# One of q's seven block products split again into seven products of blocks of half the size

## The chip, the cores and the metric

The kernel runs on one core of a Trainium2 chip. The metric is the device time in microseconds (us) of one execution. Besides that time there is a profile of one execution, in which every instruction has a start and a duration. Its engines are PE (TensorE, matrix products; PEld is the loading of its weights), DVE (VectorE), ACT (ScalarE), POOL (GpSimd) and SP (the engine that issues the DMAs here).

## The reference

Two graph layers on 64 batch elements of 256 nodes and 512 features, all in float32. The change touches one step of the second layer, the projection of its normalised input to queries.

```
h = maximum(_layernorm(x), 0)                 # x: (64, 256, 512)
x = x + concatenate([alpha @ (h @ W), h @ W]) # layer 0, alpha = masked softmax of a[0], a[1] scores
h = maximum(_layernorm(x), 0)
q = split_heads(h @ Wq.T + bq)                # 8 heads of 64
k = split_heads(h @ Wk.T + bk)
v = split_heads(h @ Wv.T + bv)
scores = einsum('bhqd,bhkd->bhqk', q, k) / 8;  masked by adj, softmax
x = x + (attn @ v merged) @ Wo.T + bo
```

## The kernel before

**Groups and stages.** The 64 batch elements are taken in 32 groups of two (`GB = 2`, `NG = 32`), so a group has 512 tokens. Three groups are in flight at once. While group g is in attention, group g+1 is projected to q, k and v (`project`, L850), and group g+2 goes through the first layer (`first_layer`, L705). The order is written out by hand in two strings (`steps`, L1182), one for each batch element b of group g. Each letter takes one piece of work: S scores, m one multiplication of softmax weights by the mask, u one product of the projection, s one piece of the first layer, o one product of the output projection, n a piece of normalisation, f a piece of the row sums ("fold"). The string for b = 0 begins `Smmnfuuuumonmnuofuusssosff`, so the seven products of q (the first seven u) stand in it, and right behind them the first products of the first layer (s).

**Order on the engines.** The matrix products run in the order in which they are written (`in_order`, L131). On VectorE, ScalarE and GpSimd, `not_sooner` (L123) keeps an instruction behind the one written before it; a scheduler places the rest. Nearly all lines of a profile read L137 (`matmul`) or L35 (every other operation), so they are told apart by the names of tiles.

**A product as seven products of half-size blocks.** q of one group is a 512 x 512 matrix times 512 tokens. It is cut into four blocks by halves of the inner dimension and of the tokens, and computed by seven products of 256 x 256 blocks instead of eight (`projection`, L857; `seven`, L534; the sums of the weights in `weight_sums`, L253). Product i multiplies one of the operands a11, a12, s4, a22, s1, s2, s3 by one of seven forms of the weight. The sums s1, s2, s3 (written over a21) and s4 come from four subtractions and additions on GpSimd (`operand_sums`, L525), named `sums` and `hT` in the profile. The products are made in the order 1, 2, 6, 7, 5, 4, 3. Products 1, 6, 5 and 3 add up in one PSUM bank, `first`, and 7 and 4 in another, `second`. In between, ScalarE copies partial results out (`kept`, L904) and VectorE adds them to the outputs:

```
L927        product(second, 4, False)
L928        vector.tensor_add(part(1, 0), second, p16)
L930        product(first, 3, False)
L931        take(part(0, 1), first, 1)
```

One such product is four matmul calls of a 128 x 128 weight by 256 columns. A float32 call leaves two records in the profile, so it is a run of 8 records. Product 3 of q has the weight block `W22`, the operand s4, and is shown as `pq<-sums,wq_sb`. `take` is two activations on ScalarE (`q<-pq,bq_sb`), which add the bias.

**What follows in the same stretch.** The first layer's products (`first_products`, L636, tile `ph`) have the same shape of scheme with 129 columns: in the order 1, 2, 6, 7, 5, 4, 3, `first` holding 1, 6, 5, 3. Before product 3 may add to `first`, VectorE must have taken product 5 out of it (L694, `H<-ph,kept_h`). Their operand sums (tiles `sums_r`, `sums_xn`, `hT`) are four more operations on GpSimd.

**VectorE and GpSimd around it.** For each batch element VectorE multiplies the softmax weights by the mask in four instructions of 128x1024 (`mask_pairs`, L970, `p<-p,maskT`). GpSimd adds the two halves of each (L983, `p<-p`). The sums of the softmax rows go through DRAM and come back as `parts` (`fold`, L990): GpSimd adds `parts` in two instructions (L1016), VectorE transposes and reduces them (L1020 to L1023). GpSimd's order in this stretch is: four `sums` operations, four `p<-p` additions, four operations for the first layer, two `parts` additions.

**Rings of buffers.** `mm` (L109) takes one of 5 PSUM banks in turn, `held_bank` (L112) a bank of its own. The tag `kept` has 3 SBUF buffers in turn.

Of the kernel before, what the change touches and what calls it, by code (L numbers as in the profile page):

```python
# [14 lines left out]
P = 128  # L15
# [42 lines left out]
def bounded(  # L58
# [37 lines left out]
    NQ = D // DH // QH  # L96
    S = 32
    scale = 1.0 / DH**0.5

    const = ctx.enter_context(tc.tile_pool(name="const", bufs=1))  # L100
    big = ctx.enter_context(tc.tile_pool(name="big", bufs=2))
# [56 lines left out]

    load(0, 0)

    square_ones = const.tile([P, P], F32, name="square_ones")
    gpsimd.memset(square_ones, 1.0)
    ident = const.tile([P, P], F32, name="ident")
    make_identity(nc, ident)
    maskT = const.tile([P, NT, N], mybir.dt.uint8, name="maskT")
    bad = const.tile([P, 2, NT], F32, name="bad")
# [86 lines left out]
    def weight_sums(name, engine=vector):  # L253
        w = w_sb[name]
        not_sooner(engine, "tensor_sub", w[:, :, T3, :], w[:, :, W22, :], w[:, :, W12, :])
        engine.tensor_sub(w[:, :, T1, :], w[:, :, W12, :], w[:, :, W11, :])
        engine.tensor_sub(w[:, :, T2, :], w[:, :, W22, :], w[:, :, T1, :])
        engine.tensor_sub(w[:, :, T4, :], w[:, :, W21, :], w[:, :, T2, :])

    def first_weight_sums():  # L260
        w11, w12, w21, w22 = (
# [31 lines left out]
    def judge():  # L293

        part = const.tile([P, 10], F32, name="part")
        vector.memset(part, 0.0)
        room = att.tile([P, 2 * HP + 1, P], F32, tag="p", name="room", bufs=1)  # L300
        heads = room[:, 2 * HP, :]
        vector.memset(heads, 0.0)
        for j in range(2):
            vector.memset(heads[j * DH : (j + 1) * DH, j * DH : (j + 1) * DH], 1.0)
        power = {}

        def bank(name):
            return mm(name).rearrange("p (h o) -> p h o", h=HP)

        for n, name in enumerate(("q", "k")):  # L310
            gram = bank(f"gram_{name}")
            for hp in range(HP):
                half, cols = hp // 2, slice(hp % 2 * P, (hp % 2 + 1) * P)
                for c in range(HP):
                    w = w_sb[name][:, c % 2, c // 2 * 2 + half, cols]
                    matmul(gram[:, hp, :], w, w, start=(c == 0), stop=(c == HP - 1))
            power[name] = room[:, n * HP : (n + 1) * HP, :]
            not_sooner(
                vector, "tensor_mul", power[name], gram, heads[:, None, :].to_broadcast([P, HP, P])
            )  # L320
            yield
        squared = {}
        for i in range(2):
            for n, name in enumerate(("q", "k")):
                square = bank(f"square_{name}{i}")
                for hp in range(HP):
                    a = power[name][:, hp, :]
                    matmul(square[:, hp, :], a, a, start=True, stop=True)
                if i < 1:
                    squared[name] = square  # L330
                else:
                    scalar.activation(
                        power[name], square, AF.Square, accum_out=part[:, 8 + n : 9 + n]
                    )
                yield
            for name, square in squared.items():
                not_sooner(scalar, "copy", power[name], square)
            if squared:
                squared.clear()
                yield  # L340

        def squares(col, *srcs):
            sums = small.tile([P, HP], F32, tag="sums", name=f"sums{col}", bufs=2)
            room = att.tile([P, D], F32, tag="kept", name=f"squares{col}", bufs=3)
            for i, src in enumerate(srcs):
                to = room[:, : src.free_size()]
                if len(src.shape) == 3:
                    to = to.rearrange("p (a b) -> p a b", a=src.shape[1])
                not_sooner(
                    scalar, "activation", to, src, AF.Square, accum_out=sums[:, i : i + 1]  # L350
                )
            vector.reduce_sum(part[:, col : col + 1], sums[:, : len(srcs)], axis=AX.X)

        squares(2, *[w0_sb[:, c, :] for c in range(HP)])
        yield
        squares(3, *[w_sb["v"][:, :, i, :] for i in range(HP)])
        yield
        for i in range(2):
            squares(i, w0_sb[:, :, i])
        yield  # L360
        squares(4, bcol["q"])
        squares(5, bcol["k"])
        squares(6, bv_col)
        vector.reduce_max(part[:, 7:8], bad.rearrange("p a t -> p (a t)"), axis=AX.X)
        yield
        total = mm("total")[:, :10]
        matmul(total, square_ones, part, start=True, stop=True)
        norm = const.tile([P, 10], F32, name="norm")
        vector.tensor_scalar(norm, total, 1e-30, None, op0=ALU.add)
        power = const.tile([P, 10], F32, name="power")  # L370
        gpsimd.memset(power, 0.5)
        gpsimd.memset(power[:, 7:8], 1.0)
        gpsimd.memset(power[:, 8:10], 1.0 / 16)
        gpsimd.tensor_tensor(norm, norm, power, op=ALU.pow)
        norms_found.append(norm)
        yield
# [3 lines left out]
    def conclude():  # L380
        (norm,) = norms_found
        root = float(D) ** 0.5


        changed = 3.0**0.5

        test = const.tile([P, 5], F32, name="test")
        side = const.tile([P, 2], F32, name="side")
# [23 lines left out]
        held = const.tile([P, 1], F32, name="held")  # L412
# [444 lines left out]
    def projection(g, name, ops):  # L857
# [69 lines left out]
        product(second, 4, False)  # L927
        vector.tensor_add(part(1, 0), second, p16)  # L928
        yield
        product(first, 3, False)  # L930
        take(part(0, 1), first, 1)  # L931
        yield

    def value_differences(g, b):
# [202 lines left out]
    def run(part):  # L1137
        for _ in part:
            pass
# [44 lines left out]
    for g in range(NG):  # L1184
        products = project(g + 1) if g + 1 < NG else iter(())
        pieces = first_layer(g + 2) if g + 2 < NG else iter(())
        for b, parts in enumerate(steps):
# [10 lines left out]
            i, count = -1, sum(part not in "frv" for part in parts)  # L1198
            for part in parts:
                i += part not in "frv"  # L1200
                if part == "u":
                    next(products, None)
# [4 lines left out]
                elif part == "n":  # L1207
                    next(norms, None)
                elif part == "m":
                    next(masks)  # L1210
                elif part == "f":
                    next(folds, None)
                    continue
                elif part == "r":
                    next(additions, None)
                    continue
                elif part == "v":
                    if g < NG - 1:
                        value_differences(g, b)
                    continue  # L1220
                else:
                    waiting = (g, b, scores(g, b))
                    masks = mask_pairs(waiting[2], g == NG - 1)
                    folds = fold(*waiting)
# [6 lines left out]
                        load(g + 3, b)  # L1231
                if b == 1 and i == 8 and g >= 2:
                    next(verdict, None)
        run(products)
        run(pieces)
    run(late)
# [5 lines left out]
def any_inputs(  # L1242
# [27 lines left out]
    TOK = GB * N  # L1270
    NG = B // GB
    scale = 1.0 / DH**0.5

    const = ctx.enter_context(tc.tile_pool(name="any_const", bufs=1))
    setup = ctx.enter_context(tc.tile_pool(name="any_setup", bufs=1))
# [333 lines left out]
```

## Time and profile before

| what | value |
|---|---|
| time, median of 3 runs | 2383.98 us (2383.02 to 2384.33) |
| time of the profiled execution | 2383.11 us |
| its span in the profile | 2381.5 us |
| PE busy | 2369.8 us (100%) |
| PEld busy | 1998.5 us (84%) |
| DVE busy | 1695.2 us (71%), 3347 instructions |
| POOL busy | 1421.3 us (60%), 1288 instructions |
| ACT busy | 1016.6 us (43%) |
| granted TensorE clock | 1.0 |

The span is what lies between the first and the last instruction; the profiled execution's own time is 1.6 us more. Each row of a timeline gives the start in us from the start of the span, the duration in us, the engine, the line, the operation, the tiles written and read, the shape and the number of merged instructions; a bracket at the end gives the engine's idle time before it and what ended it. PE's busy time is a modelled one: a run of 8 records of 256 columns is shown as 1.89 us, and the next run starts 1.73 us after it.

### The profile page before, as it was taken

The page shows a single profiled execution, that of the slowest core. Times are in us where ns is not written, and L with a number is a line of the kernel's source. Part 1 is how long each engine was busy: PE and PEld are TensorE (multiplying, and loading weights), DVE is VectorE, ACT ScalarE, POOL GpSimd, SP SyncE. Part 2 cuts the span into 40 slices and gives each one's busy share as a digit, 9 for nine tenths or more (in the row PEclk, how much of TensorE's full clock was granted, in tenths as well). Part 3 has the DMA queues.
Part 4 walks back from the last instruction along what each step waited for, and adds up shares of the span by engine and source line. Part 5 has one row for each costly group of instructions (what it writes and reads, how often), then busy time and mean ns, then how long its engine had stood idle before and what let it go on. Part 6 is the DMA issues. An engine that isn't in the chain of part 4 may idle for free.

```text
span 2381.5 us, 43080 instructions
## 1 busy us (share of the span) xinstructions
PE 2369.8 (100%) x15828; PEld 1998.5 (84%) x15828; DVE 1695.2 (71%) x3347; ACT 1016.6 (43%) x2017; POOL 1421.3 (60%) x1288
## 2 busy tenths in 40 slices
PE   9999999999999999999999999999999999999998
PEld 8888888888888888888888888888888888888886
DVE  7577676776766776767777667776677676677666
ACT  5444444443443444444444434444444444343431
POOL 4575665666656555666656575566665565656551
PEclk9999999999999999999999999999999999999999
DMA  5344445444445544454444455444544445554331
GB/s 186 128 148 146 140 137 162 151 150 149 138 141 157 167 146 138 138 157 154 142 147 142 151 155 168 141 136 139 162 151 147 141 143 156 153 157 146 110 106 46
DMA packets 271865, 343.50 MB, mean 144 GB/s; under 512 B 25376, under 2 KB 217120, under 8 KB 271648
## 3 DMA queue, kind: packets, MB, share of 16 engines
q1 hardware_dynamic: 271648, 340.69, 46.2%
q8 instruction: 126, 2.06, 0.4%
q14 instruction: 91, 0.75, 0.1%
HBM read 176.95 MB, written 163.64 MB: 143 GB/s over the span
## 4 chain that ended last, share of the span: by engine, by line
PE 97%; DVE 1%; POOL 1%; DMA 1%; issue 0%; ACT 0%; SPq 0%; ACTq 0%; POOLq 0%; DVEq 0%
PE pq L137 16%; PE pk L137 16%; PE py L137 16%; PE pv L137 16%; PE sc L137 10%; PE pr L137 9%; PE ph L137 8%; PE po L137 5%; DMA x<-in_x_dram 0%; POOL parts L35 0%; PE total L137 0%; DVE x L35 0%; PE gram_q L137 0%; PE gram_k L137 0%; DVE prod L35 0%
## 5 line engine op out<-in xcount | busy, mean ns | idle before, releaser
L35 POOL TENSOR_TENSOR p<-p 128x512 f32<-128x512 f32 x248 | 388.3, 1579 | 460.2 <-DVE p L35 456.5
L35 DVE TENSOR_TENSOR p<-p,maskT 128x1024 f32<-128x1024 f32 x256 | 333.1, 1322 | 3.2 <-ACT p L35 3.2
L35 ACT ACTIVATE p<-sc 128x512 f32<-128x512 f32 x512 | 257.8, 627 | 148.8 <-PE sc L137 144.1
L35 DVE TENSOR_TENSOR x<-py,x 128x256 f32<-128x256 f32 x448 | 185.1, 413 | 186.4 <-PE py L137 180.2
L35 ACT ACTIVATE xn<-x,factor 128x512 f32<-128x512 f32 x256 | 194.7, 807 | 284.1 <-POOL factor L35 276.6
L35 POOL TENSOR_TENSOR parts<-parts 128x512 f32<-128x512 f32 x248 | 247.7, 999 | 74.0 <-DMA parts<-rows 52.1
L137 PE MATMUL py<-wo_sb,oT 128*128 128x256 f32 x1024 | 262.4, 379 | 0.6 <-DVE oT L35 0.6
L137 PE MATMUL pk<-hT,wk_sb 128*128 128x256 f32 x1024 | 244.8, 382 | 0.0
L137 PE MATMUL pq<-hT,wq_sb 128*128 128x256 f32 x1024 | 240.1, 382 | 1.1 <-ACT hT L35 0.7
L137 PE MATMUL sc<-q,k 64*128 64x256 f32 x2048 | 239.5, 383 | 0.1
L137 PE MATMUL pv<-wv_sb,hT 128*128 128x256 f32 x1024 | 236.8, 379 | 0.0
L137 PE MATMUL pr<-p,v 128*32 128x256 f32 x4096 | 234.2, 380 | 0.0
L137 PEld LDWEIGHTS sc<-q,k 64*128 64x128 f32 x2048 | 193.3, 187 | 46.8 <-issue 26.3
L35 POOL TENSOR_TENSOR factor<-factor,rexp 128x2 f32<-128x2 f32 (+1 forms) x132 | 118.0, 894 | 187.3 <-DVE factor L35 187.0
L137 PEld LDWEIGHTS pq<-hT,wq_sb 128*128 128x128 f32 x1024 | 191.8, 190 | 36.7 <-issue 10.3
L137 PEld LDWEIGHTS py<-wo_sb,oT 128*128 128x128 f32 x1024 | 194.2, 190 | 28.2 <-DVE oT L35 1.1
L137 PEld LDWEIGHTS pk<-hT,wk_sb 128*128 128x128 f32 x1024 | 189.7, 190 | 33.3 <-issue 9.9
L137 PEld LDWEIGHTS pv<-wv_sb,hT 128*128 128x128 f32 x1024 | 194.6, 190 | 26.5
L137 PEld LDWEIGHTS pr<-p,v 128*32 128x32 f32 x4096 | 126.7, 110 | 97.8 <-issue 15.9
L137 PE MATMUL py<-wo_sb,o_sums 128*128 128x256 f32 x768 | 197.6, 380 | 0.5 <-DVE x L35 0.5
L137 PE MATMUL pv<-wv_sb,sums 128*128 128x256 f32 x768 | 181.6, 379 | 0.3 <-DVE v L35 0.3
L137 PE MATMUL pk<-sums,wk_sb 128*128 128x256 f32 x768 | 181.5, 379 | 0.0
(149 smaller groups left out, 4058.7 us busy)
## 6 DMA issues: line engine op xcount, KB each, us to landing
passed<-xt SPq DMA_DIRECT2D x124, 512.0 KB, 3.1
moved<-passed SPq DMA_DIRECT2D x496, 128.0 KB, 3.4
rows<-p SPq DMA_DIRECT2D x124, 512.0 KB, 3.4
parts<-rows SPq DMA_DIRECT2D x496, 128.0 KB, 3.0
x<-in_x_dram SPq DMA_DIRECT2D x64, 512.0 KB, 4.4
out_dram<-x SPq DMA_DIRECT2D x62, 512.0 KB, 4.0
own<-line SPq DMA_DIRECT2D x30, 256.0 KB, 3.1
wq_sb<-in_L_gnn_Wq_dram SPq DMA_DIRECT2D x2, 512.0 KB, 9.2
```

Source lines behind the costliest of these rows:

```text
L35: instruction = getattr(self.engine, operation)(*args, **kwargs)
L137: in_order(nc.tensor.matmul(*args, **kwargs))
```

## The change

From group 2 on (`FINER = 2`), product 3 of q alone is made by seven products of 128 x 128 blocks, by the same scheme once more. Its operand s4 and its weight `W22` are cut into four blocks each. What is new:

- `finer_weight_sums` makes three sums of blocks of the weight and writes a fourth over one of them: four VectorE instructions of 128x128, once, in group 0 at b = 1.
- `finer_sums` makes four sums of blocks of the operand, four VectorE instructions of 128x128 in each group, at the third mask multiplication of b = 0 (the m after four u).
- `finer_product` replaces `product(first, 3)` and `take`. Products 2, 4 and 3 of the small blocks add straight onto quarters of `first`. Products 1 and 7 go to a new PSUM bank, and ScalarE copies both out in one instruction (128x256, tile `saved_q`). Product 6 is added onto product 1 in that bank and copied (128x128), then product 5, and copied. VectorE adds the copies, the bias and `first` in two instructions of 128x256, and the seventh product with a third. `saved_q` is a fourth buffer per group of the ring `kept`.
- `tails` puts small product 6 behind the first s after the seventh u, and small product 5 behind the second s.

Apart from this, the constants `square_ones` and `ident` move to one tile, `early`, that shares its place with a later one, and a few small tiles of the check on the inputs shrink from 128 to 32 partitions.

```diff
-    square_ones = const.tile([P, P], F32, name="square_ones")
+    early = big.tile([P, 2, P], F32, tag="oT1", name="early", bufs=1)
+    square_ones, ident = early[:, 0], early[:, 1]
...
+    def finer_weight_sums(name):
+        w11, w12, w21, w22 = finer_blocks(name)
+        made = big.tile([P, 3, P], F32, tag="finer", name=f"finer_{name}", bufs=1)
+        t1, t2, t4 = (made[:, i] for i in range(3))
+        not_sooner(vector, "tensor_sub", t1, w12, w11)
+        vector.tensor_sub(t2, w22, t1)
+        vector.tensor_sub(t4, w21, t2)
+        not_sooner(vector, "tensor_sub", w12, w22, w12)
+        finer[name] = {1: w11, 2: w21, 3: w22, 4: t4, 5: t1, 6: t2, 7: w12}
...
+    def finer_sums(g, s4):
+        a11, a12, a21, a22 = (
+            s4[:, c, m * P : (m + 1) * P] for m in range(2) for c in range(2)
+        )
+        sums = big.tile([P, 4, P], F32, tag="s4", name=f"s4_{g}", bufs=1)
+        s1, s2, s3, s4 = (sums[:, i] for i in range(4))
+        not_sooner(vector, "tensor_add", s1, a21, a22)
+        not_sooner(vector, "tensor_sub", s2, s1, a11)
+        not_sooner(vector, "tensor_sub", s3, a11, a21)
+        not_sooner(vector, "tensor_sub", s4, a12, s2)
+        finer_operands[g] = {1: a11, 2: a12, 3: s4, 4: a22, 5: s1, 6: s2, 7: s3}
+        yield
...
+        if name == "q" and g >= FINER:
+            tail = finer_product(g, name, first, part(0, 1))
+            next(tail)
+            tails.append([tail, 2, 1, 2])
+            yield
+            return
         product(first, 3, False)
         take(part(0, 1), first, 1)
...
+    def finer_product(g, name, first, to):
+        weights, by = finer[name], finer_operands[g]
+        bank = mm(f"p{name}3_{g}")
+        x1, x7 = bank[:, :P], bank[:, P : 2 * P]
...
+        saved = att.tile([P, 4, P], F32, tag="kept", name=f"saved_{name}_{g}", bufs=3)
...
+        product(quarter(first, 0, 0), 2)
+        product(quarter(first, 0, 1), 4)
+        product(quarter(first, 1, 0), 3)
+        product(x1, 1, True)
+        product(x7, 7)
+        scalar.copy(saved[:, :2].rearrange("p i n -> p (i n)"), bank[:, : 2 * P])
+        yield
+        product(x1, 6)
+        scalar.copy(saved[:, 2], x1)
+        yield
+        product(x1, 5)
+        scalar.copy(saved[:, 3], x1)
+        for o, made in ((0, saved[:, 0:3:2]), (1, saved[:, None, 3].to_broadcast([P, 2, P]))):
+            both = [of[:, o].rearrange("p (m n) -> p m n", m=2) for of in (to, first)]
+            add(both[0], o, both[1], made)
+        upper = to[:, :, P:]
+        vector.tensor_add(upper, upper, saved[:, None, 1].to_broadcast([P, 2, P]))
+        yield
...
+                if (g, b) == (FINER - 2, 1) and part in "suo" and i == 20:
+                    finer_weight_sums("q")
...
                 elif part == "m":
                     next(masks)
+                    if i >= 4:
+                        next(fine, None)
...
+                if part in "suo" and tails:
+                    tail = tails[0]
+                    tail[1] -= 1
+                    if tail[1] == 0:
+                        next(tail[0])
+                        tail[1] = tail[2]
+                        tail[3] -= 1
+                    if tail[3] == 0:
+                        tails.pop(0)
```

More of the change, by code (lines that the diff above doesn't have):

```diff
@@ L98, in bounded @@
     scale = 1.0 / DH**0.5
+    FINER = 2
     const = ctx.enter_context(tc.tile_pool(name="const", bufs=1))
@@ L159, in bounded @@
     load(0, 0)
-    square_ones = const.tile([P, P], F32, name="square_ones")
+    early = big.tile([P, 2, P], F32, tag="oT1", name="early", bufs=1)
+    square_ones, ident = early[:, 0], early[:, 1]
     gpsimd.memset(square_ones, 1.0)
-    ident = const.tile([P, P], F32, name="ident")
     make_identity(nc, ident)
@@ L258, in weight_sums, with finer_blocks @@
         engine.tensor_sub(w[:, :, T4, :], w[:, :, W21, :], w[:, :, T2, :])
+    finer = {}
+    def finer_blocks(name):
+        w = w_sb[name][:, :, W22, :]
+        return [w[:, c, o * P : (o + 1) * P] for c in range(2) for o in range(2)]
+    def finer_weight_sums(name):
[7 more added lines that the diff above has]
+        finer[name] = {1: w11, 2: w21, 3: w22, 4: t4, 5: t1, 6: t2, 7: w12}
+    finer_operands = {}
+    def finer_sums(g, s4):
[10 more added lines that the diff above has]
+        yield
+    tails = []
     def first_weight_sums():
@@ L365, in judge @@
         yield
-        total = mm("total")[:, :10]
-        matmul(total, square_ones, part, start=True, stop=True)
-        norm = const.tile([P, 10], F32, name="norm")
+        total = mm("total")[:S, :10]
+        matmul(total, ones, part, start=True, stop=True)
+        norm = const.tile([S, 10], F32, name="norm")
         vector.tensor_scalar(norm, total, 1e-30, None, op0=ALU.add)
-        power = const.tile([P, 10], F32, name="power")
+        power = const.tile([S, 10], F32, name="power")
         gpsimd.memset(power, 0.5)
@@ L385, in conclude @@
         changed = 3.0**0.5
-        test = const.tile([P, 5], F32, name="test")
-        side = const.tile([P, 2], F32, name="side")
+        test = const.tile([S, 5], F32, name="test")
+        side = const.tile([S, 2], F32, name="side")
         not_sooner(vector, "tensor_add", test[:, 0:1], norm[:, 0:1], norm[:, 1:2])
@@ L411, in conclude @@
         vector.tensor_scalar(test, test, 1.0, None, op0=ALU.is_le)
-        held = const.tile([P, 1], F32, name="held")
+        held = const.tile([S, 1], F32, name="held")
         vector.tensor_reduce(held, test, axis=AX.X, op=ALU.min)
@@ L929, in projection, with product, quarter, add @@
         yield
+        if name == "q" and g >= FINER:
[4 more added lines that the diff above has]
+            return
         product(first, 3, False)
         take(part(0, 1), first, 1)
+        yield
[3 more added lines that the diff above has]
+        x1, x7 = bank[:, :P], bank[:, P : 2 * P]
+        def product(out, i, start=False):
+            matmul(out, weights[i], by[i], start=start, stop=True, skip_group_check=True)
+        def quarter(of, o, m):
+            return of[:, o, m * P : (m + 1) * P]
+        saved = att.tile([P, 4, P], F32, tag="kept", name=f"saved_{name}_{g}", bufs=3)
+        def add(out, o, of, i):
+            vector.scalar_tensor_tensor(
+                out, of, bcol[name][:, 2 + o : 3 + o], i, op0=ALU.add, op1=ALU.add
+            )
+        product(quarter(first, 0, 0), 2)
[15 more added lines that the diff above has]
+        vector.tensor_add(upper, upper, saved[:, None, 1].to_broadcast([P, 2, P]))
         yield
@@ L1198, in bounded @@
             i, count = -1, sum(part not in "frv" for part in parts)
+            fine = iter(())
+            if FINER <= g + 1 < NG and b == 0:
+                fine = finer_sums(g + 1, operands[g + 1][3][0])
             for part in parts:
+                if (g, b) == (FINER - 2, 1) and part in "suo" and i == 20:
+                    finer_weight_sums("q")
                 i += part not in "frv"
@@ L1272, in any_inputs @@
     scale = 1.0 / DH**0.5
+    FINER = 2
     const = ctx.enter_context(tc.tile_pool(name="any_const", bufs=1))
```

## The prediction

> **What bounds the kernel now.** I read the page's chain of waits first, then the timeline of one steady group engine by engine, then the one group that takes longer.
>
> ```profile
> PE 97%; DVE 1%; POOL 1%; DMA 1%; issue 0%; ACT 0%; SPq 0%; ACTq 0%; POOLq 0%; DVEq 0%
> ```
>
> PE sets the end and hardly waits. So a change is worth what it takes from PE's stream, minus every wait it puts into it. The chain in order of time shows one period per group:
>
> ```profile
> 159.37 7.10 PE pq L137 x32
> ...
> 233.14 7.10 PE pq L137 x32
> ...
> 306.12 7.10 PE pq L137 x32
> ```
>
> The usual period is 72.98 us (306.12 - 233.14); the one before it is 73.77, 0.79 more. I come back to it.
>
> **PE's gain.** From PE's timeline:
>
> ```profile
> 20.05 3.75 PE L137 MATMUL gram_q<-wq_sb 128*128 128x128 f32 x32
> 23.63 3.64 PE L137 MATMUL po<-H,e 128*128 128x257 f32 x16
> ...
> 1048.89 1.89 PE L137 MATMUL pq<-sums,wq_sb 128*128 128x256 f32 x8
> 1050.62 1.95 PE L137 MATMUL ph<-w_sb,hT 128*128 128x129 f32 x16
> ```
>
> The start of the next run gives the pitch. Old product 3: 1050.62 - 1048.89 = 1.73 for 8 records, 216 ns each. Records of 128 columns: (23.63 - 20.05)/32 = 112 ns. The new product is seven calls, 14 records: 14 x 112 = 1.57. Gain 0.16 us a group, in 30 groups 4.8 us, 0.20% of the time. That is all there is to win.
>
> The Trainium skill (TensorE: Matmul & The Clock Gate, Back-to-back issue gap) speaks against small blocks: it gives 81 ns for a load-and-multiply pair of 128 columns and 131 ns for one of 512, so the time falls far less than the columns. Estimated along that line, 256 columns would take 98 ns, and 14 small pairs 1.13 us against 0.78 for 8, a loss. The rows of this trace (float32) show 112 against 216, so I keep the gain.
>
> **ScalarE and PE's two new waits.** Two activations (0.84 together) become copies of 256, 128 and 128 columns. Small product 6 must wait for the first copy, 5 for the second. Rows: a copy of 258 columns took 0.37, the smallest activations (4 columns) 0.20, so one of 128 lies between; I take 0.27. From the end of a PE run to ScalarE's start is 0.20 to 0.25 in the copies of `ph`. The s between takes 8 x 0.112 = 0.90 on PE. First copy: 0.25 + 0.37 + 0.12 back to PE = 0.74, against 0.90 less 0.11 (weights load one record ahead) = 0.79: just hidden. The second copy queues behind `kept_h` and is hidden by about 0.1. I cost both at nothing; uncovered they would cost at most some 0.3 a group. In the last group (31) there is no first layer any more, so the changed program has both products directly behind each other: 0.8 and 0.7 of bare waiting, **1.5 us once**.
>
> **VectorE's new work.** Four 128x128 operations, two of 128x256 out of PSUM (row with a scalar operand and PSUM: 0.48 us) and one addition of 128x256: about 2.5 us a group, on an engine that is busy 71%. Averages hide what matters, the moment. The four operand sums stand between the third mask multiplication and the first `x<-py` addition:
>
> ```profile
> 1041.17 1.69 DVE L35 TENSOR_TENSOR p<-p,maskT 128x1024 f32<-128x1024 f32 x1
> 1044.77 0.42 DVE L35 TENSOR_TENSOR x<-py,x 128x256 f32<-128x256 f32 x1 [1.92 <-PE py L137]
> 1045.11 1.22 DVE L35 TENSOR_TENSOR p<-p,maskT 128x1024 f32<-128x1024 f32 x1
> ```
>
> There are 1.92 us of idle time. No row shows 128x128: it lies between 0.17 (factor, 2 columns) and 0.42 (256 columns); by 0.28 four make 1.1 and would fit. But these have both operands in SBUF, and such an operation does not run beside GpSimd:
>
> ```profile
> 1036.56 1.49 DVE L35 TENSOR_TENSOR oT<-oT 128x256 f32<-128x256 f32 x1
> ...
> 1071.74 0.42 DVE L35 TENSOR_TENSOR oT<-oT 128x256 f32<-128x256 f32 x1
> ```
>
> The same instruction took 0.42 with GpSimd idle, 1.49 when it met GpSimd's 1.45 us `sums` of 1036.31. In these rows each ends when the other has finished; they take turns. And GpSimd is busy in just that gap:
>
> ```profile
> 1039.59 5.62 POOL L35 TENSOR_TENSOR p<-p 128x512 f32<-128x512 f32 x3 [1.83 <-DVE p L35]
> 1046.47 1.27 POOL L35 TENSOR_TENSOR p<-p 128x512 f32<-128x512 f32 x1 [1.26 <-DVE p L35]
> ...
> 1052.72 2.07 POOL L35 TENSOR_TENSOR parts<-parts 128x512 f32<-128x512 f32 x2
> ```
>
> Walk through it. GpSimd's second `p<-p` runs until 1043.98. Sum 1 ends 0.15 behind it (128 columns), 1044.13. The third `p<-p`, already waiting, takes 1.13: 1045.26. Sum 2, which needs sum 1, ends at 1045.42, 3 and 4 by 1045.82. `x<-py` follows from 1045.74, the fourth mask multiplication from 1046.09 instead of 1045.11: **0.97 late**. The fourth `p<-p` waits for it, and behind that GpSimd runs without a gap to `parts`, so `parts` is 0.97 late too. The new addition `q<-q,saved_q` (both in SBUF) comes at about 1053.3, in the middle of that work, and pushes it by another 0.2. So `parts` ends 1.16 late.
>
> **Who waits for that.** VectorE's order is `parts` transposed, reduced, then `H<-ph`:
>
> ```profile
> 1054.83 0.45 DVE L35 STREAM_TRANSPOSE parts<-parts 128x256 f32<-128x256 f32 x1
> 1055.31 0.42 DVE L35 TENSOR_REDUCE compact<-parts 128x8 f32<-128x256 f32 x1
> 1056.21 0.43 DVE L35 TENSOR_TENSOR H<-ph,kept_h 128x258 f32<-128x258 f32 x1 [0.48 <-PE ph L137]
> ```
>
> The first-layer product 3 waits for this `H`. There is 0.48 idle ahead of it; PE comes 0.16 earlier now, and two VectorE instructions overlap by 0.07, so 0.39 of lateness is free: stall 1.16 - 0.39 = 0.77. That this chain costs PE its full lateness is in the trace already, in the period of 73.77, where `parts` came 1.36 later than usual:
>
> ```profile
> 178.80 0.45 DVE L35 STREAM_TRANSPOSE parts<-parts 128x256 f32<-128x256 f32 x1 [1.42 <-POOL parts L35]
> ...
> 180.15 0.97 PEld L137 LDWEIGHTS ph<-w_sb,sums_xn 128*128 128x128 f32 x8 [0.74 <-issue]
> ```
>
> **How often.** Groups differ. In 12 of the 29 groups that have both the change and the first layer (timeline around 1111 to 1121, for one), GpSimd has finished its second addition (1115.13) before the third mask multiplication ends (1116.21). There only the third is in the way, the delay is 0.25 and the stall about 0.04. In 16 the order is that walked above; their second addition ends at different times, and the walk gives stalls of 0.3 to 1.3, 0.68 on average. The one left is that of 73.77.
>
> **Once, at the start.** The four weight sums stand in group 0 behind the reduction at 143.12, where GpSimd's `x<-x` (143.33 to 144.60) holds them: some 2.1 on VectorE, in front of transposes, statistics and the `v<-pv` addition at 147.01, for which v's product 3 at 148.81 waits. Stall about 1.2. The DMA of the transposes (`passed`, 146.85) goes behind four others of SP's queue that end at 146.76, and is 0.1 late. With the next group, late already, I take **2 us**; ends 0 and 4.
>
> SP's order and its DMAs are the same in the changed program. `early`, the 32 partitions and the fifth bank's turn cost nothing: the bank that a new one follows was emptied many us before.
>
> **Sum.** -30 x 0.16 = -4.8; 16 x 0.68 = +10.9; 12 x 0.04 = +0.5; start +2.0; last group +1.5: +10.1. On the profiled execution's 2383.11 us (span 2381.5 and 1.6 around it) this gives **2393.2 us**. That execution lies 0.9 below the median of 2383.98, well inside what is uncertain here.
>
> **Rivals.**
>
> *The gap hides the sums* (not slower). VectorE's 1.92 idle takes all four because they are short enough to slip between GpSimd's additions, or because GpSimd wins less often than in the walk. It decides at 0.39 us of lateness in `parts`. For it: 128 columns are half of any row that I have. Against: the stall of 0.74 above and the rows of 1.49. Then -4.8 + 1.5 = -3.3, up to +0 with part of the start: 2379.8 to 2383. Chance 0.18.
>
> *Mostly the short order.* The longer period gives GpSimd's sums more time, and nearly all groups fall into the order of 1111: -4.8 + 29 x 0.04 + 2 + 1.5 = 0: 2383 to 2388. Chance 0.13.
>
> *Always the long order.* The new lateness keeps every group in it, or the two copies miss their 0.1 as well: 29 x 0.68 to 29 x 1.0 with the one-time costs and the gain, +18 to +28: 2401 to 2411. Chance 0.14.
>
> *Forecast*, a mixture: 2388 to 2401. Chance 0.55.
>
> **Numbers.** About 0.2% (4.8 us) is what a measurement of this kernel can tell from no change. Faster by more than that, below 2379.2, is left for the rival's best end: 0.05. Within: the rest of it and most of the short order: 0.26. Slower: 0.69. The range takes in the hidden case and most of the long order: 2379.5 to 2405.
>
> **What would show it.** Right: `pq` of 128 columns at 112 ns; the third period and later ones at 73.4 to 73.9 instead of 72.98 in about half the groups, 72.9 in the others; the four `s<-sums` at 1.3 us where they meet GpSimd; `ph<-w_sb,sums_xn` with idle time ended by DVE `H`. Wrong: a steady period of 72.82 (72.98 - 0.16), which is the first rival; idle time of PE ahead of `pq<-s,finer_q` ended by ScalarE in more than the last group, which would mean that the copies are late.

## The result and the profile after

The changed kernel takes 2393.0 us (median of 6 runs, 2391.28 to 2394.6), the kernel before 2383.97 (6 runs). The ratio is 1.0038, 95% interval [1.0025, 1.0051]: slower by 9 us. The profiled execution took 2392.57 us, its span is 2390.9 (before: 2381.5).

The busy times and the chain of waits on the page of the changed kernel:

```profile
PE 2371.2 (99%) x16008; PEld 2002.3 (84%) x16008; DVE 1816.4 (76%) x3561; ACT 1013.4 (42%) x2047; POOL 1419.8 (59%) x1288
...
PE 87%; DVE 5%; POOL 3%; DMA 2%; issue 2%; SPq 0%; ACT 0%; POOLq 0%; DVEq 0%; ACTq 0%
```

PE's part of the chain has fallen from 97% to 87%; VectorE, GpSimd and the DMA stand in it now. PE's waits by what ended them (total us, times, longest). The line of a matmul is L138 in the changed kernel, where it was L137:

```profile
PE ph L138 <- DVE H L35: 6.0, 13, 1.3
PE pv L138 <- DVE v L35: 2.2, 1, 2.2
PE py L138 <- DVE x L35: 1.2, 3, 0.8
...
PE pq L138 <- ACT saved_q L35: 0.8, 2, 0.5
```

Before, the first of these was 0.6 in one place and the second 0.3 in one; the second is all in group 6, to which I come back. In the first halves of groups 2 to 29 (the table below) the trace shows no idle time of PE but that ahead of the first-layer product that needs `H`. The chain in order of time has the starts of q's products:

```profile
825.55 7.10 PE pq L138 x32
898.36 7.10 PE pq L138 x32
971.58 7.10 PE pq L138 x32
1044.40 7.10 PE pq L138 x32
...
1409.41 7.10 PE pq L138 x32
1483.00 7.10 PE pq L138 x32
```

Periods of 72.81 (the old 72.98 less the gain of 0.16), 73.22, 72.82 and 73.59: some groups have only the gain, others a stall as well.

One stalled group on VectorE (start, duration, out<-in, idle time and what ended it):

```profile
536.44 1.35 DVE L35 TENSOR_TENSOR s<-sums 128x128 f32<-128x128 f32 x1
537.83 1.25 DVE L35 TENSOR_TENSOR s<-s,sums 128x128 f32<-128x128 f32 x1
539.00 0.28 DVE L35 TENSOR_TENSOR s<-sums 128x128 f32<-128x128 f32 x1
539.20 0.28 DVE L35 TENSOR_TENSOR s<-sums,s 128x128 f32<-128x128 f32 x1
539.40 0.41 DVE L35 TENSOR_TENSOR x<-py,x 128x256 f32<-128x256 f32 x1
539.73 1.21 DVE L35 TENSOR_TENSOR p<-p,maskT 128x1024 f32<-128x1024 f32 x1
...
549.62 0.45 DVE L35 STREAM_TRANSPOSE parts<-parts 128x256 f32<-128x256 f32 x1 [1.11 <-POOL parts L35]
550.10 0.42 DVE L35 TENSOR_REDUCE compact<-parts 128x8 f32<-128x256 f32 x1
550.44 0.76 DVE L35 TENSOR_TENSOR H<-ph,kept_h 128x258 f32<-128x258 f32 x2
```

GpSimd's second and third `p<-p` additions run from 535.39 to 538.92. The first two sums wait for them in turn, the other two, with GpSimd idle, take 0.28. The mask multiplication comes late, then `parts`, then `H`, and on PE product 3 of the first layer:

```profile
549.67 1.06 PE L138 MATMUL ph<-w_more,hT 128*128 128x129 f32 x8
551.00 1.13 PE L138 MATMUL ph<-w_sb,sums_xn 128*128 128x129 f32 x8 [0.27 <-DVE H L35]
```

The usual step from one such run to the next is 0.89 (the run before these two starts at 548.78, the first of them at 549.67); here it is 1.33, a stall of 0.44.

**Where the 9.4 us of span are.** From the starts of the score products S on PE, every group falls into two halves (b = 0 and b = 1), so two executions can be laid beside each other piece by piece. The first half of group g holds the new product for group g+1. The table holds all kernels of this study. The medians are times; the kernel before had 2383.9 to 2384.8 beside them. The other columns are the differences of the profiled execution to that of the kernel before, in us:

| kernel | median, us | start, to first S | group 0 | group 1, b=0 | b=0, groups 2 to 29 | b=1, group 6 | other b=1 | groups 30, 31 and end |
|---|---|---|---|---|---|---|---|---|
| changed | 2393.0 | +2.0 | +1.1 | +0.45 | +3.0 | +2.0 | 0 | +0.9 |
| changed, again | 2392.96 | +0.2 | +1.3 | +0.2 | +5.8 | +1.8 | 0 | +1.15 |
| one_input | 2383.74 | -0.2 | +1.1 | -0.5 | -4.4 | +3.3 | 0 | +1.1 |
| sums_out | 2382.59 | -0.1 | +1.1 | -0.4 | -4.8 | +0.85 | 0 | +1.1 |
| sums_only | 2388.58 | -0.1 | 0 | +1.5 | +5.4 | 0 | 0 | -0.1 |
| fold_later | 2425.98 | +0.3 | +1.1 | -0.5 | -4.65 | +1.6 | +43.4 | +1.6 |
| once | 2389.66 | 0 | 0 | +2.1 | +4.3 | -0.9 | 0 | +0.2 |
| between | 2394.9 | -0.1 | 0 | +0.4 | -3.8 | -0.4 | +15.0 | +0.2 |
| mask_first | 2399.94 | -0.2 | 0 | +2.1 | +13.9 | -0.9 | 0 | -0.2 |
| from_psum | 2379.67 | +0.2 | 0 | +0.8 | -3.3 | -0.9 | 0 | -0.1 |
| from_psum_x7 | 2379.56 | +0.3 | 0 | +1.6 | -4.2 | -0.9 | 0 | -0.1 |

PE's gain alone would be 28 x -0.16 = -4.5 in the column of the first halves. So the changed kernel's stalls there are 3.0 + 4.5 = 7.5 us, and 10.3 in its second profiled execution.

Two entries hold something else as well: the +3.3 of one_input in group 6, and in fold_later's +43.4 the second half of group 28 (4.7 over its usual length). In each there are 3.41 us in which PE's granted clock was half (0.50), from 591.59 us in the one and from 2205.41 in the other, where PE had just waited for 1.93 and 2.46 us.

### The profile page after: what moved, and what is told of

The parts are those of the page before. It is cut to its first block, busy times and chain, and to the rows that moved or that the text cites. A ratio compares the mean times of both kernels' runs of the same rounds, so it can differ in the third digit from the quotient of the medians.

```text
span 2390.9 us, 43626 instructions
## 1 busy us (share of the span) xinstructions
PE 2371.2 (99%) x16008; PEld 2002.3 (84%) x16008; DVE 1816.4 (76%) x3561; ACT 1013.4 (42%) x2047; POOL 1419.8 (59%) x1288
## 4 chain that ended last, share of the span: by engine, by line
PE 87%; DVE 5%; POOL 3%; DMA 2%; issue 2%; SPq 0%; ACT 0%; POOLq 0%; DVEq 0%; ACTq 0%
PE pk L138 16%; PE pv L138 15%; PE py L138 15%; PE pq L138 12%; PE pr L138 9%; PE sc L138 9%; PE ph L138 6%; PE po L138 4%; POOL parts L35 1%; DMA parts<-rows 1%; DVE p L35 1%; DVE o_sums L35 1%; POOL p L35 1%; POOL sums_xn L35 1%; DVE s L35 0%
## 5 line engine op out<-in xcount | busy, mean ns | idle before, releaser
L138 PE MATMUL py<-wo_sb,oT 128*128 128x256 f32 x1024 | 262.5, 379 | 1.4 <-DVE x L35 0.8
L138 PE MATMUL pk<-hT,wk_sb 128*128 128x256 f32 x1024 | 244.9, 382 | 0.0
L138 PE MATMUL pq<-hT,wq_sb 128*128 128x256 f32 x1024 | 240.1, 382 | 1.1 <-ACT hT L35 0.7
L138 PE MATMUL sc<-q,k 64*128 64x256 f32 x2048 | 238.9, 383 | 0.1
L138 PE MATMUL pv<-wv_sb,hT 128*128 128x256 f32 x1024 | 236.8, 379 | 0.0
L138 PE MATMUL pr<-p,v 128*32 128x256 f32 x4096 | 234.2, 380 | 0.0
L138 PEld LDWEIGHTS sc<-q,k 64*128 64x128 f32 x2048 | 193.1, 187 | 46.5 <-issue 26.3
L138 PEld LDWEIGHTS pq<-hT,wq_sb 128*128 128x128 f32 x1024 | 191.8, 190 | 36.7 <-issue 10.3
L138 PEld LDWEIGHTS py<-wo_sb,oT 128*128 128x128 f32 x1024 | 194.1, 190 | 29.4 <-DVE x L35 1.2
L138 PEld LDWEIGHTS pk<-hT,wk_sb 128*128 128x128 f32 x1024 | 189.7, 190 | 33.3 <-issue 9.9
L138 PEld LDWEIGHTS pv<-wv_sb,hT 128*128 128x128 f32 x1024 | 194.6, 190 | 26.5
L138 PEld LDWEIGHTS pr<-p,v 128*32 128x32 f32 x4096 | 126.8, 110 | 97.8 <-issue 14.9
L138 PE MATMUL py<-wo_sb,o_sums 128*128 128x256 f32 x768 | 197.7, 380 | 0.5 <-DVE x L35 0.5
L138 PE MATMUL pv<-wv_sb,sums 128*128 128x256 f32 x768 | 181.6, 379 | 2.2 <-DVE v L35 2.2
L138 PE MATMUL pk<-sums,wk_sb 128*128 128x256 f32 x768 | 181.5, 379 | 0.0
```

The costliest lines, as they stand in the source:

```text
L138: in_order(nc.tensor.matmul(*args, **kwargs))
```

## The experiments

The theory is that of the prediction: a VectorE operation with both operands in SBUF takes turns with GpSimd; four such sums delay the fourth mask multiplication, and through `parts` and `H` PE. The rivals: it is the added work of VectorE as such, or PE waits for ScalarE's copies.

**The same number of operations, with one operand each.**

```diff
-not_sooner(vector, "tensor_add", s1, a21, a22)
-not_sooner(vector, "tensor_sub", s2, s1, a11)
-not_sooner(vector, "tensor_sub", s3, a11, a21)
-not_sooner(vector, "tensor_sub", s4, a12, s2)
+not_sooner(vector, "transpose", s1, a21)
+not_sooner(vector, "transpose", s2, s1)
+not_sooner(vector, "transpose", s3, a11)
+not_sooner(vector, "transpose", s4, s2)
```

> The four operand sums on VectorE become four 128x128 transposes of one operand each, in the same places (so product 3 of q multiplies other numbers than it should). The number of VectorE instructions and roughly their busy time stay; what goes is only that an operation has two operands in SBUF. Theory (turns with GpSimd make parts, then H, then PE late; the stalls of the b=0 halves are worth about 7.5 us): stalls ahead of ph<-w_sb,sums_xn nearly gone, most periods 72.82, 2385 to 2387.5 us. Rival (VectorE's added busy time makes H late): unchanged, 2391.5 to 2394.5 us.

2383.74 us, ratio to the kernel before 1.0001 [0.9992, 1.0010]; 1.3 below the theory's range. The instructions of the tile `s` on VectorE (min/median/max ns), first in the changed kernel, then here:

```profile
L35 DVE TENSOR_TENSOR s<-sums x60: 276/279/1358, 169.2 to 2294.2; 128x128 f32<-128x128 f32 x60
L35 DVE TENSOR_TENSOR s<-s,sums x30: 1240/1286/1332, 170.6 to 2293.0; 128x128 f32<-128x128 f32 x30
L35 DVE TENSOR_TENSOR s<-sums,s x30: 277/279/281, 171.9 to 2294.4; 128x128 f32<-128x128 f32 x30
```

```profile
L35 DVE STREAM_TRANSPOSE s<-sums x60: 267/284/304, 167.0 to 2283.9; 128x128 f32<-128x128 f32 x60
L35 DVE STREAM_TRANSPOSE s<-s x60: 266/292/314, 167.3 to 2284.1; 128x128 f32<-128x128 f32 x60
```

Alone such an operation takes 0.28 us either way. With two operands in SBUF the second sum took 1.24 to 1.33 in each of 30 groups, with one never over 0.31. VectorE has as many instructions in both kernels (3561), and 27 of 28 first halves have the pure gain, 36.87 (column -4.4 against the -4.5 above). The rival of busy time falls.

**No sums at all.**

```diff
-sums = big.tile([P, 4, P], F32, tag="s4", name=f"s4_{g}", bufs=1)
-s1, s2, s3, s4 = (sums[:, i] for i in range(4))
-...
+s1, s2, s3, s4 = a21, a12, a11, a22
```

> The four operand sums are left out; blocks of the operand stand in for them (so product 3 of q multiplies other numbers than it should). PE, ScalarE and the three additions of the new product stay. Theory: about what one_input gives, 2385 to 2387 us, since it is not the 1.1 us of work but the turns that cost. Rival (busy time): less is taken away than the whole added time, 1.1 of 2.5 us of VectorE a group, so about 4/9 of the 7.5 us: 2389 to 2391 us, and clearly below one_input.

2382.59 us, ratio 0.9995 [0.9986, 1.0004]; 2.4 below the theory's range and 6.4 below the rival's. The first halves give -4.8 against -4.4 of one_input: taking the work away as well adds next to nothing to taking away the turns. The other 2.5 us between the two spans stand in group 6, part of them in one_input's stretch of half clock.

**The sums alone, in the kernel before.**

```diff
-if name == "q" and g >= FINER:
+if False:
...
-if (g, b) == (FINER - 2, 1) and part in "suo" and i == 20:
-    finer_weight_sums("q")
```

> The four operand sums are made, but nothing reads them: product 3 of q is the old one with its two activations, and there are no weight sums. It is the kernel before with the sums alone. Theory: the sums alone delay parts by up to 1 us in groups of the long order; without PE's gain the free lateness is 0.16 larger, without q<-q,saved_q the lateness is 0.2 smaller: stalls of 3 to 7 us in all, 2387 to 2391 us. Rival (the copies and the three additions of the new product cost, not the sums): 2383.5 to 2385 us, periods of 72.98.

2388.58 us, ratio 1.0019 [1.0010, 1.0028]. Four sums that nobody reads cost 4.7 us by the medians. In the profiled execution, which took 2389.8, the whole loss is in first halves (+5.4, and +1.5 in group 1). PE's waits there:

```profile
PE ph L138 <- DVE H L35: 3.4, 8, 1.0
```

The same wait as in the changed kernel. Together with sums_out, from the other side: the sums make the stalls; the copies, the added additions and the small products do not.

**The place where the lateness reaches PE: the fold behind the H additions.**

```diff
-"Smmnfuuuumonmnuofuusssosffsssuvno..."
+"Smmnfuuuumonmnuofuusssosfssfsuvno..."
```

> The changed kernel with the second summing of the fold (parts transposed and reduced, and the transfer of the next parts) moved behind the two H additions on VectorE in the first halves; some statistics behind it change places with it. Nothing of the sums is changed, parts are as late as they were. Theory: H no longer waits for parts, stalls ahead of ph<-w_sb,sums_xn gone, periods 72.82, 2385 to 2387.5 us, unless the second transfer of parts, now about 1.3 us later, becomes late itself. Rival (PE waits for something else, the copies or VectorE's load in general): 2391.5 us or more.

2425.98 us, ratio 1.0180 [1.0166, 1.0194]: the worst of all, and still half of the theory holds. The four sums wait for GpSimd as before (up to 1.36 us), but the first halves are at 36.87 (column -4.65) and PE waits for `H` no more; `parts` hurt through that one place. The number lies in the rival's range, but not for the rival's reason: the second halves became 0.8 to 2.5 longer in every group, and 4.7 in the one with the half clock, +43.4 outside group 6. Most of it is in S, which takes 4.96 us on average there instead of 3.65. The second half of one of them, on GpSimd, ScalarE and PE:

```profile
1083.27 2.08 POOL L35 TENSOR_TENSOR parts<-parts 128x512 f32<-128x512 f32 x2 [2.45 <-DMA parts<-rows]
```

```profile
1086.36 1.71 ACT L35 ACTIVATE e<-own,H 128x256 f32<-128x256 f32 x4 [2.02 <-issue]
...
1089.36 4.00 ACT L35 ACTIVATE p<-sc 128x512 f32<-128x512 f32 x8
```

```profile
1087.78 2.00 PE L138 MATMUL sc<-q,k 64*128 64x256 f32 x16
1089.99 2.26 PE L138 MATMUL sc<-q,k 64*128 64x256 f32 x16 [0.21 <-ACT p L35]
```

The second `parts` is transferred later, and GpSimd sits idle for 2.45 us until it lands. `parts` and `e` share one buffer (tag "e", one of it), so ScalarE writes `e` later, and the exponentials of the scores (`p<-sc`) stand behind `e` on ScalarE. S waits for them: 20.5 us in 26 places. A wait was taken away from PE and a larger one was put in its place.

**Half that way, with three edits outside the steady groups.** The kernel "once" has these three alone:

```diff
-if name == "q" and g >= FINER:
+if name == "q" and FINER <= g < NG - 1:
...
-if FINER <= g + 1 < NG and b == 0:
+if FINER <= g + 1 < NG - 1 and b == 0:
...
-if (g, b) == (FINER - 2, 1) and part in "suo" and i == 20:
+if (g, b) == (FINER - 2, 1) and part in "suo" and i == 31:
...
-if b == 1 and i == 8 and g >= 2:
+if (b, i) == (1, 8) and 2 <= g < 6 or (g, b, i) == (7, 0, 31):
```

> The changed kernel with three edits outside the steady groups: the last group (31) keeps the old product 3 of q; the weight sums stand later in group 0, after the last v additions; the summing of the verdict's norms, with its 1.95 us operation on GpSimd, moves from the second half of group 6 to the end of the first half of group 7. Theory (last group 1.2, weight sums 1.1, second half of group 6 2.85 above its usual 35.95, and the half clock of 16.75 to 20.16 us of the profiled execution by chance and not by the change): start 85.5 instead of 87.6, these three places at their usual lengths, the stalls of the first halves as they were, in all 2384 to 2387.5 us. Rival (one of the three costs the same wherever it stands, or the half clock belongs to the changed start): 1 to 3 us more, at that place.

2389.66 us, ratio 1.0024 [1.0013, 1.0034], 2.2 above the theory's range. The last group gave its 1.2 back, group 0 its 1.1, group 6 is at 35.95. But group 1 is 1.6 longer than in the changed kernel (40.46 against 38.82), so the weight sums' stall was not saved: as much comes back one half later. sums_only, without weight sums, has +1.5 there too, and from_psum_x7 below, in which no sum takes a turn, +1.6, with PE waiting 1.3 us for `H`. So the turns alone do not explain this group, and what does is open.

"between" moves the fold behind one H addition only:

```diff
-"Smmnfuuuumonmnuofuusssosffsssuvno..."
+"Smmnfuuuumonmnuofuusssosfsfssuvno..."
```

> The edits of once, and the second summing of the fold moved behind one H addition (that of product 5) instead of two as in fold_later; some statistics change places with it. The second transfer of parts is then issued about 1.1 us later than in the changed kernel, against 2.1 in fold_later. Theory: first halves 36.87 as in fold_later; what decides is whether parts free the buffer that e needs before ScalarE wants to write e. If so, second halves 35.95 and 2377 to 2380 us; if not, second halves up to 1.2 above that and 2385 to 2410 us.

2394.9 us, ratio 1.0046 [1.0033, 1.0060]. First halves at 36.87 except for three, second halves 36.43 instead of 35.95 nearly everywhere: +15.0, a third of fold_later's. The lateness that PE does not see in the first half it sees in the second. At this place, too, the one wait is exchanged for the other.

**The mask multiplication first, then the sums.**

```diff
-"Smmnfuuuumonmnuofuusssosffsssuvno..."
+"Smmnfuuuummonnuofuusssosffsssuvno..."
...
+if b == 0 and 9 <= i <= 14:
+    next(fine, None)
```

> The edits of once, and on VectorE the fourth mask multiplication in front of the operand sums instead of behind them, the sums spread over the next steps. GpSimd then gets its fourth addition without the wait; the sums still take turns with it. Theory: parts are no later than before, stalls ahead of ph<-w_sb,sums_xn gone, first halves 36.87, 2377 to 2381 us; the sums themselves end later, and the q additions behind them, which PE feels only if a bank of pq or an s comes late. Rival (the sums cost wherever they stand, since GpSimd has no gap behind the fourth multiplication): PE waits for s or for q at the new place, 0.3 to 1 us a group, 2385 us or more.

2399.94 us, ratio 1.0068 [1.0054, 1.0081]: the rival. PE's waits, and the sums in a group:

```profile
PE pq L138 <- DVE q L35: 13.3, 19, 2.5
```

```profile
1052.43 1.36 DVE L35 TENSOR_TENSOR s<-sums 128x128 f32<-128x128 f32 x1
1053.71 0.41 DVE L35 TENSOR_TENSOR x<-py,x 128x256 f32<-128x256 f32 x1
1054.04 1.03 DVE L35 TENSOR_TENSOR s<-s,sums 128x128 f32<-128x128 f32 x1
1055.00 0.28 DVE L35 TENSOR_TENSOR s<-sums 128x128 f32<-128x128 f32 x1
1055.20 1.35 DVE L35 TENSOR_TENSOR s<-sums,s 128x128 f32<-128x128 f32 x1
1056.47 0.68 DVE L35 TENSOR_TENSOR q<-pq,kept_q 128x512 f32<-128x512 f32 x1
```

The stalls for `H` are gone, as expected. But here GpSimd has no gap, three of the four sums wait for their turn, and the addition of `q` behind them releases its PSUM bank late. At both places that were tried the turns came with the sums; between them `x<-py,x`, with one operand in PSUM, takes its 0.41 with GpSimd at work.

**One operand from PSUM.** That row suggests the way out: ScalarE, with a gap of 2.6 us at the place, copies the operand block to a bank of PSUM.

```diff
+bank = mm(f"blocks_{g}").rearrange("p (c n) -> p c n", c=2)
+not_sooner(scalar, "copy", bank, s4)
+b11, b12, b21, b22 = (bank[:, c, m * P : (m + 1) * P] for m in range(2) for c in range(2))
...
-not_sooner(vector, "tensor_add", s1, a21, a22)
-not_sooner(vector, "tensor_sub", s2, s1, a11)
-not_sooner(vector, "tensor_sub", s3, a11, a21)
-not_sooner(vector, "tensor_sub", s4, a12, s2)
+not_sooner(vector, "tensor_add", s1, a21, b22)
+not_sooner(vector, "tensor_sub", s2, s1, b11)
+not_sooner(vector, "tensor_sub", s3, b11, a21)
+not_sooner(vector, "tensor_sub", s4, b12, s2)
```

> The edits of once, and the four operand sums read one operand from PSUM: ScalarE copies the 128x512 operand block there (some 0.56 us, in a gap of 2.6 us between two kept_q), and each sum takes its second block from that bank. The number, size and place of the sums on VectorE are unchanged. Theory (a VectorE operation takes turns with GpSimd only if both operands lie in SBUF; x<-py,x with one in PSUM took 0.42 while GpSimd worked): sums of about 0.28 us each also where they meet GpSimd, first halves 36.87, span 2375.5 to 2378 us, 2377.5 to 2380.5 us by the median. Rival (VectorE's place in the gap is too short whatever the operands, or the bank held for the copy makes PE wait for its next one): 2384 us or more, with waits of PE for pq or H.

2379.67 us, ratio to the kernel before 0.9982 [0.9973, 0.9991]: faster than both. Two of the four sums in all groups, one group's first sum beside GpSimd's work, and what the chain says:

```profile
L35 DVE TENSOR_TENSOR s<-s,blocks x29: 286/286/289, 167.8 to 2208.3; 128x128 f32<-128x128 f32 x29
L35 DVE TENSOR_TENSOR s<-blocks,sums x29: 281/282/284, 168.0 to 2208.5; 128x128 f32<-128x128 f32 x29
```

```profile
528.13 5.63 POOL L35 TENSOR_TENSOR p<-p 128x512 f32<-128x512 f32 x3 [1.83 <-DVE p L35]
...
531.32 0.27 DVE L35 TENSOR_TENSOR s<-sums,blocks 128x128 f32<-128x128 f32 x1
```

```profile
PE 95%; DVE 2%; DMA 1%; POOL 1%; issue 0%; ACT 0%; SPq 0%; ACTq 0%; POOLq 0%; DVEq 0%
```

The same four sums in the same places, none over 0.29, with GpSimd at work for at least three quarters of their time in each of the 29 groups. Against "once", which differs only in ScalarE's copy, its bank and where one operand lies, the first halves lose 7.6 us (+4.3 to -3.3) and group 1 another 1.3 (but only 0.5 in from_psum_x7). Of PE's gain of 4.5 there, 1.1 is still lost, most of it in two groups. Of the 4.2 us below the kernel before, 0.9 belong to the moved verdict, which that kernel could have as well.

**The last addition from PSUM too.**

```diff
-vector.tensor_add(upper, upper, saved[:, None, 1].to_broadcast([P, 2, P]))
+vector.tensor_add(upper, upper, x7[:, None, :].to_broadcast([P, 2, P]))
```

> As from_psum, and the last addition of the new product, q<-q,saved_q, reads its 128 columns from the PSUM bank of the small products instead of the copy in SBUF. Theory: this addition, 0.8 to 1.5 us where it met GpSimd, takes about 0.42; the prediction gave it 0.2 us of lateness of parts, which the free 0.39 covers once the sums are out of the way: no difference to from_psum beyond 1 us. Rival (that addition has its own share in the stalls): another 1 to 5 us less.

2379.56 us, ratio 0.9980 [0.9971, 0.9989]: no difference to from_psum, though the addition itself took 0.42 in all 29 groups instead of 0.86 to 1.54. The first halves of groups 2 to 29 are 0.9 shorter, that of group 1 is 0.8 longer. Its share of lateness lies under the free 0.39, as the theory had it, or is too small to be told here.

**The changed kernel a second time.**

> The changed kernel itself once more, for a second profiled execution. Theory: first S at 85.4 to 85.9 us, since the half clock of 16.75 to 20.16 us in the first profile is a matter of chance, and a span about 2 us shorter, 2388.5 to 2389.5; first halves stalled by 6 to 9 us in all, in other groups than before; the second half of group 6 again 1.5 to 4 us above its usual length. Rival (the half clock belongs to the changed start): first S at 87.6 again. By the median 2391 to 2394 us either way.

2392.96 us, ratio 1.0036 [1.0023, 1.0049]; the span of 2391.9 is 2.4 above the theory's, and the stalls of the first halves, 10.3, are above its 6 to 9. The start is at its usual length (+0.2). The granted clock in the stretch around 17 us (columns: stretch, length, busy time of PE, PEld, DVE, ACT, POOL with instructions, clock, DMA share, GB/s), first profile, then second:

```profile
17.00:18.00 1.00, 1.00 (x3) 0.73 (x3) 0.96 (x3) 0.00 (x0) 0.00 (x0) 0.50 1.14 306
```

```profile
17.00:18.00 1.00, 1.00 (x7) 0.86 (x6) 0.96 (x3) 0.08 (x1) 0.00 (x0) 1.00 1.21 277
```

Half the clock in the one, the full clock in the other, with the same program; in the ten other profiles it is 1.00 in this stretch as well. So a half clock there is not what this program always meets, and the +2.0 at the start of the first profile is not counted to the change. The stalls of the first halves were 10.3 here against 7.5; one group with 2.0, which had 0.93 in the first profile, makes up for part of that. The expectation had said "in other groups than before". They are largely the same ones: the 14 groups that lose time through two waiting sums in the first profile come back here but for one, with two others.

## Why the prediction was right, point by point

The prediction said 2393.2, the measurement 2393.0. That the two are 0.2 apart is luck: three terms were too large (the sums, the start, the last group), one cost of 2 us was not seen, and the stalls alone differ by 2.8 between two executions of the same program. What is right is the sign, the range and the chain of waits.

- **PE's gain**: 0.16 us a group, right. The groups without a stall have 72.81 or 72.82 instead of 72.98.
- **ScalarE's copies at nothing**: right. PE waits for `saved_q` twice in the whole execution, in the last group, 0.8 us. The last group's net cost was put at 1.5 - 0.16 = 1.34 and measured 1.18 (31.94 against 30.75).
- **The sums and their turns**: the chain was right link by link. one_input, sums_out and from_psum take away the turns, the work, and the turns again, and the stalls nearly all go each time; sums_only brings them in alone; fold_later shows that they reach PE through `H` at product 3.
- **How often**: the term that was mis-sized. Forecast were 16 groups of 0.68 and 12 of 0.04, 11.4 us; measured were 7.5 and 10.3. The first sum tells the order of a group: it took 1.35 in the long order and 0.28 in the short one. In the first profile 14 groups are in the long order, with 0.14 to 0.93 each, 0.52 on average; in the second 15, with 0.66 on average. So the number of groups was nearly right, and one stall was put too high, by a quarter in the first profile. Which groups they are was not right: the prediction counted the orders of the kernel before, and 10 of the 28 groups have changed theirs, six to the short order and four to the long one. What moves them was not tried and stays open.
- **The start at 2**: measured 1.1 in group 0 and 0.45 in group 1 (1.3 and 0.2 the second time). The weight sums took 2.16 us on VectorE, as forecast (2.1). But PE does not wait for `v` there, as the prediction had it; it waits for the addition `x` of the output projection, which comes behind the weight sums and the transposes:

```profile
149.17 1.13 PE L138 MATMUL py<-wo_sb,oT 128*128 128x256 f32 x4 [0.79 <-DVE x L35]
```

- **Group 6**: not seen. The second half of the group in which the verdict's norms are summed (GpSimd `norm`, 1.95 us) was 0.86 over its length before; after, 2.85 and 2.6. In "once", where that operation stands elsewhere, the half has its 35.95. The added 2 us are PE's wait of 2.23 for `v`. They begin with the transfer `rows<-p`, which is issued 16.1 us behind the start of this half in each kernel that has the operation there except fold_later, and lands at different times. Rows for the five microseconds from there, first before, then after; for `rows<-p` with its number, KB and us from issue to landing, for a load of instructions with number, MB and share of the DMA engines:

```profile
rows<-p SPq DMA_DIRECT2D x1, 512.0 KB, 3.2
```

```profile
q8 instruction: 1, 0.02, 2.1%
...
rows<-p SPq DMA_DIRECT2D x1, 512.0 KB, 5.0
```

The next transfers of SP's queue wait for this one, `passed` lands 2 us later, and so do the transposes, `parts` and `v`. While the rows are on their way, instructions are loaded over the DMA in the changed kernel (both profiles: 5.0 us to landing), in one_input (5.0) and in sums_out (4.1); none are in the kernel before and in sums_only (3.2 in both), which do not have the growth. So it is neither the smaller constants nor the turns of the sums. That the loads hold up the rows is my reading of these six traces; no run moved a load.

The terms as measured: -4.8 + 7.5 to 10.3 + 1.6 + 1.3 + 1.9 = 7.5 to 10.3 us, around the measured 9.

**The rivals.** The gap does not hide the sums: the second sum waited in all 30 groups. Mostly the short order: half true in the count, but the stalls left are 7.5 us and more, not 1. Always the long order: no; 12 groups have no stall at all in the first profile, and 11 in the second.

## What to carry to other kernels

An operation on an engine with idle time is not free if it needs something that another engine holds: look at what the other engine does in that very gap, and at who stands in its queue. Where two engines take turns over operands in SBUF, try an operand in PSUM before moving the operation; moved, it took its turns along here. And a wait that is moved off the bound engine should be followed to the buffer that it frees: here `parts` and `e` shared one.

## What the runs showed of the hardware

A 128x128 float32 operation of VectorE took 0.28 us with both operands in SBUF and GpSimd idle, 1.02 to 1.37 when it met a GpSimd addition, and 0.27 to 0.29 with one operand in PSUM and GpSimd at work. The Trainium skill (SBUF — State Buffer, SBUF: two separate sides) describes an exclusive lock between a VectorE operation with two SBUF inputs and a GpSimd operation that reads SBUF, held for the whole instruction; these rows agree with it.

PE's clock, once full, went back to half for 3.41 us at 16.75 us in one execution of the changed kernel, with PE at work on both sides and no wait over 0.24 us in the 12 us ahead of it, and cost the start 2 us; in the second profile of the same program it did not. The same 3.41 us stand in one_input and fold_later less than half a microsecond behind waits of 1.93 and 2.46 us. But in group 6 of the changed kernel's two profiles PE waited 2.23 and 2.00 us and the granted clock stayed at 1.00. So the length of one wait does not tell by itself whether the clock falls.
